# Seven block products at the end of batch 1, and variances by quarters, in a two-layer attention kernel

## The chip, the cores and the metric

The kernel runs on one core of one Trainium2 chip. The metric is the device time of one execution in microseconds (us), from the first to the last instruction of the program with what lies around them. A median of several runs is given. The engines are named as in the profile: PE multiplies matrices, PEld loads its weights, DVE and POOL work on tiles in SBUF, ACT evaluates activation functions, SP issues most of the DMAs. PE, DVE, ACT and POOL each execute their instructions in the order in which the program emits them. A DMA that SP issues waits in SP's own queue until its source is written.

## The reference

The input is x, two batches of 512 channels by 2048 tokens (64 x 32), in float32. Layer 0 is softmax attention with 8 heads over all tokens, an output projection and a residual. Layer 1 is landmark attention with a pseudoinverse, then a feed-forward map whose two matrices have no nonlinearity between them. Each half of layer 1 begins with a normalization over the channels and adds its result to what it got:

```python
def _ln_t(v, eps=1e-5):
    m = jnp.mean(v, axis=-1, keepdims=True)
    s = jnp.var(v, axis=-1, keepdims=True)
    return (v - m) / jnp.sqrt(s + eps)
...
x = _L0_conv_ref(x, Wq, Wk, Wv, Wout, bout)          # attention, projection, + x
t = _to_tokens(x)
t = t + _L1_attn_ref(_ln_t(t), Wqkv, Wout, bout, conv_w)
...
out = out @ Wout + bout                               # the end of _L1_attn_ref
...
t = t + _L1_ffn_ref(_ln_t(t), qidx, scales, W)
...
y = jnp.einsum('bsd,od->bso', x, w_lora)              # in _L1_ffn_ref
out = jnp.einsum('bsd,od->bso', y, W)
```

## The kernel before

Channels lie on partitions, as four chunks of 128 (KC = 4); tokens are worked on in four blocks of 512 (NTB = 4, TB = 512). The heads of a batch are four pairs (NPAIR = 4). A product of a 512x512 weight with a block of 512 tokens is 16 products of 128x128 with 128x512; each product in float32 leaves two matmul records and two weight loads in the profile.

The program goes through these stages, and each has its filler, work of another stage that is put between its steps so that PE has something to do while other engines answer.

1. Layer 0, `attention0`: eight pairs of heads. Steps are made in groups of two (`GROUP`): scores on PE, exponentials on ACT into a pool of six tiles (`ppool`), sums of them on DVE (L1307), values on PE. After given groups (`BURSTS`) the filler gets a burst; after others one small call is taken from the list `soon`. While the first pair of batch 1 runs, the filler is `finish0_units`, the end of batch 0: for each block of 512 tokens the output projection (`out0_units`, four units of four products, L1168, each evacuated by DVE at L1175 from one of two PSUM banks "pp"), then the steps of `norm0_steps`. Those are: sums over the channels on DVE, the mean by a product with a matrix of 1/512 on PE (L1190), the subtraction on DVE, squares on ACT, their sums on DVE, the variance by the same kind of product (L1206) with a square root on ACT (L1208); then, taken from `soon` after one group, the reciprocal on DVE (L1227), and from `soon` after the next group the two multiplications with it, one half on POOL (L1230) and one on DVE (L1231), and the store of the normalized block.
2. The end of batch 1 of layer 0 beside the first products of layer 1. The order is a string written out by hand, `ORDER`: m is a step of the products, n a step of the norms, o a unit of a projection. These products already are seven block products instead of eight (`Unit`, `products`).
3. Batch 1's products in layer 1, and values.
4. The main loop of layer 1 over eight pairs, batch 1's four first (n = 0 to 3), then batch 0's (n = 4 to 7). `pinv` makes five rounds on each pair, about 7.4 us of PE each (L1856, L1866) with DVE between (L1879), and calls `chunk(c)` after a round and `last(i)` six times at the end. Those hold the landmark attention of the pair after (`after`), the last attention of the pair before (`before`: `attn1_scores`, `attn1_values`, `attn1_sums`, `attn1_inverse`, `attn1_end`), and, from n = 4, units of `finish1_units`, which is the end of batch 1 in layer 1. For each block of 512 tokens that is: the projection (four units), the norm (`norm_units`, the same `statistics` as above, its reciprocal at L1988), and the map (`map_units`, four units of four products, L2022). The map works on the centred block; each of its results is multiplied by the inverse deviation (`rstd`) on DVE (L2011), added to the block (L2012) and stored from SP (L2013). `TURNS` says at which places a unit ("f") is taken; some of the generator's items are empty (`GAP`), and use a turn without any work. The fourth block is taken earlier on its own ("o").
5. The tail: the last pair's last attention (`last_attn1`), the end of batch 1 and that of batch 0 in the order of the string `TAIL` (1 is a step of the attention, f a unit of batch 1, a and b units of batch 0's first and second projection, s and t steps of their norms), and then batch 0's maps, with the norm of the next block between the units of the map of this one.

A softmax's denominators are already treated in quarters: `sums_of` (L805) puts sums over 512 columns as four products with 32 weights each on four quarters of the partitions, DVE takes the reciprocal of 128x256 instead of 128x512 (L1336, L1952), and `spread` copies the result back to all rows by eight small DMAs from SP (L816).

The copies in question:

```python
    def spread(dst, few):
        for h in range(2):
            for to in range(2):
                for j in range(2):
                    lo, src = h * D + to * Q, h * D + j * Q
                    nc.sync.dma_start(dst[lo : lo + Q, j * LM : (j + 1) * LM], few[src : src + Q, :])
```

## Time and profile before

| what | us |
|---|---|
| median of 3 runs (2648.84 to 2649.84) | 2648.89 |
| the profiled execution's own time | 2649.55 |
| its span, from the first to the last instruction | 2647.7 |
| PE idle from 690 to 900 (end of batch 0 in layer 0) | 0.0 of 210 |
| PE idle from 1350 to 1520 (the stage of `ORDER`) | 3.0 of 170 |
| PE idle from 2090 to 2480 (n = 4 to 7 of the main loop) | 4.4 of 390 |
| PE idle from 2480 to 2648 (tail) | 10.0 of 168 |
| DVE busy in the same four stretches | 135, 132, 210, 103 |

The busy share of PE is a union of records, and a record lasts longer than the time after which the next one may start: a 128x512 record takes 592 ns, and the next starts 429 ns after it. What a product costs where PE runs without a break is read from the starts of neighbouring records or weight loads, not from its duration. "Idle before" in a group is the time in which the engine had nothing just before these instructions, and the arrow names what ended it. SPq is the queue of SP, where a DMA's instruction has a duration of its own before the transfer has landed.

### The profile page before, as it was taken

How to read it: one execution, taken by the hardware profiler on the slowest of the kernel's cores; microseconds unless marked ns; L12 is line 12 of the kernel's file. 1: busy time of each engine (PE TensorE's matmuls, PEld its weight loads, DVE VectorE, ACT ScalarE, POOL GpSimd, SP SyncE). 2: the span in 40 equal slices, each digit the busy share in tenths (PEclk: the TensorE clock that was granted, in tenths of full speed). 3: DMA queues.
4: the chain of work that ended last, by engine and by line, in shares of the span. 5: the costliest groups of instructions: out<-in, count | busy, mean ns of one | idle time of the engine just before them, and what ended most of it. 6: DMA issues, size and time to landing. Idle time of an engine off the chain costs nothing.

```text
span 2647.7 us, 41440 instructions
## 1 busy us (share of the span) xinstructions
PE 2623.1 (99%) x16882; PEld 1353.3 (51%) x16882; DVE 1780.1 (67%) x2259; ACT 921.0 (35%) x1398; POOL 169.6 (6%) x127
## 2 busy tenths in 40 slices
PE   9999999999999999999999999999999999999998
PEld 5343443444344344353344555777677666665444
DVE  5788897886667778767867866544644645465665
ACT  1444453443344434435522323223333232231310
POOL 0011011000001100000002000000000000000000
PEclk9999999999999999999999999999999999999999
DMA  4011011201221201011115633213111112121211
GB/s 147 22 30 36 13 33 49 77 21 52 88 80 58 91 25 32 25 56 60 41 44 182 225 125 118 98 33 129 48 37 61 60 45 100 34 81 36 97 35 49
DMA packets 123608, 177.16 MB, mean 67 GB/s; under 512 B 16784, under 2 KB 77968, under 8 KB 120848
## 3 DMA queue, kind: packets, MB, share of 16 engines
q1 hardware_dynamic: 117264, 153.15, 17.8%
q0 software_dynamic: 5440, 20.97, 2.0%
q8 instruction: 134, 2.20, 0.4%
q14 instruction: 66, 0.54, 0.1%
q10 hardware_dynamic: 704, 0.31, 0.0%
HBM read 94.02 MB, written 63.57 MB: 60 GB/s over the span
## 4 chain that ended last, share of the span: by engine, by line
PE 91%; DVE 6%; issue 1%; ACT 1%; DMA 1%; SPq 0%; DVEq 0%; ACTq 0%
PE av_f L1319 15%; PE sc_f L1289 15%; PE pb L1866 5%; PE pa L1866 5%; PE vp_f L1153 4%; PE yp_g L1168 4%; PE yp_f L1168 4%; PE fp_g L2022 4%; PE vp L1153 4%; PE pc_f L1021 3%; PE pu L2207 3%; DVE acc_f L1307 3%; PE pu_f L1021 2%; PE sc L1695 2%; PE sc L1923 2%; PE av L1716 2%
## 5 line engine op out<-in xcount | busy, mean ns | idle before, releaser
L1297 ACT ACTIVATE p_f<-sc_f 128x1024 f32<-128x1024 f32 x512 | 496.5, 1021 | 540.2 <-PE sc_f L1289 540.0
L1307 DVE TENSOR_TENSOR acc_f<-acc_f,p_f 128x1024 f32<-128x1024 f32 x448 | 575.3, 1284 | 110.8 <-ACT p_f L1297 83.9
L1319 PE MATMUL av_f<-p_f,v_f 64*64 64x512 f32 x4096 | 494.4, 589 | 2.8 <-DVE q_f L1326 2.8
L1289 PE MATMUL sc_f<-q_f,k_f 64*64 64x512 f32 x4096 | 489.9, 591 | 0.3 <-ACT p_f L1297 0.3
L1319 PEld LDWEIGHTS av_f<-p_f,v_f 64*64 64x64 f32 x4096 | 162.5, 133 | 286.8 <-issue 274.3
L1289 PEld LDWEIGHTS sc_f<-q_f,k_f 64*64 64x64 f32 x4096 | 154.2, 133 | 282.2 <-issue 277.2
L1866 PE MATMUL pa<-M 128*128 128x192 f32 (+1 forms) x640 | 150.3, 380 | 0.0
L1866 PE MATMUL pb<-R 128*128 128x192 f32 (+1 forms) x640 | 149.3, 380 | 0.6 <-DVE M L1879 0.6
L1153 PEld LDWEIGHTS vp_f<-wv_f,x 128*128 128x128 f32 x1024 | 115.8, 192 | 5.5 <-issue 5.2
L1866 PEld LDWEIGHTS pb<-R 128*128 128x128 f32 x640 | 106.5, 190 | 23.6 <-DVE M L1879 0.8
L1866 PEld LDWEIGHTS pa<-M 128*128 128x128 f32 x640 | 108.2, 193 | 19.8 <-ACT M L1857 2.0
L1153 PE MATMUL vp_f<-wv_f,x 128*128 128x128 f32 x1024 | 117.9, 276 | 0.0
L1168 PE MATMUL yp_g<-o,wo_f 128*128 128x512 f32 x256 | 113.8, 595 | 0.0
L1168 PE MATMUL yp_f<-q_f,wo_f 128*128 128x512 f32 x256 | 112.4, 595 | 0.1
L1339 POOL TENSOR_TENSOR q_f<-q_f,rinv_f 128x512 f32<-128x512 f32 x32 | 49.0, 1530 | 970.1 <-DMA rinv_f<-acc_f 647.5
L1153 PE MATMUL vp<-w,xh 128*128 128x128 f32 x896 | 105.8, 276 | 0.0
L1153 PEld LDWEIGHTS vp<-w,xh 128*128 128x128 f32 x896 | 102.2, 192 | 5.4 <-issue 3.5
L1879 DVE SCALAR_TENSOR_TENSOR M<-M,pb 128x320 f32<-128x320 f32 (+1 forms) x160 | 60.1, 417 | 60.8 <-PE pb L1866 60.8
L2022 PE MATMUL fp_g<-xn_g,mT 128*128 128x512 f32 (+1 forms) x232 | 99.3, 579 | 0.0
L1928 ACT ACTIVATE p<-sc 128x512 f32<-128x512 f32 x128 | 66.7, 602 | 91.6 <-PE sc L1923 91.1
L1960 POOL TENSOR_TENSOR o<-o,rinv 128x512 f32<-128x512 f32 x32 | 44.4, 1386 | 772.9 <-DVE rinv L1959 587.5
L1879 DVE SCALAR_TENSOR_TENSOR R<-M,pa 128x320 f32<-128x320 f32 (+1 forms) x160 | 58.5, 407 | 42.1 <-PE pa L1866 42.1
(293 smaller groups left out, 3215.9 us busy)
## 6 DMA issues: line engine op xcount, KB each, us to landing
xh<-xh_fd SPq DMA_DIRECT2D x12, 1024.0 KB, 7.9
rinv_f<-acc_f SPq DMA_DIRECT2D x256, 32.0 KB, 1.9
xr_f<-in_x_dram SPq DMA_DIRECT2D x8, 1024.0 KB, 5.2
x_fd<-xr_f POOLq DMA_DIRECT2D x8, 1024.0 KB, 4.7
xh_fd<-xn_f POOLq DMA_DIRECT2D x8, 1024.0 KB, 4.4
k_fd<-kq SPq DMA_DIRECT2D x16, 512.0 KB, 2.6
q_fd<-kq SPq DMA_DIRECT2D x16, 512.0 KB, 3.2
k<-k_fd SPq DMA_DIRECT2D x8, 1024.0 KB, 6.0
```

The source lines that it names most:

```text
L1021: nc.tensor.matmul(to, lhsT=w[:, k, :], rhs=x[:, k, :], start=start and k == 0, stop=k == 1, skip_group_check=True,)
L1153: nc.tensor.matmul(vp[:, j * P : (j + 1) * P], lhsT=xb[:, k, j * P : (j + 1) * P], rhs=w_of(k), start=k == 0, stop=k == KC - 1,)
L1168: nc.tensor.matmul(yp, lhsT=wo_sb[:, k, m * P : (m + 1) * P], rhs=oTs[k][:, toks], start=k == 0, stop=k == NPAIR - 1,)
L1289: nc.tensor.matmul(sc[r * D : (r + 1) * D, h, :], lhsT=hd.k[rows, lo : lo + D], rhs=hd.q[rows, t * TB : (t + 1) * TB], start=True, stop=True,)
L1297: nc.scalar.activation(p, sc, AF.Exp, scale=D**-0.5)
L1307: nc.vector.tensor_tensor(acc, first if c == 1 else acc, p, ALU.add)
L1319: nc.tensor.matmul(av[r][half, :], lhsT=hd.v[keys, c, half], rhs=pp[keys, h, :], start=c == 0, stop=c == NST - 1,)
L1866: nc.tensor.matmul(dst, lhsT=lhsT[:, k, t * P : (t + 1) * P], rhs=rhs[:, k, :], start=k == 0, stop=k == 1)
L1879: nc.vector.scalar_tensor_tensor(out, m, scale, pr, ALU.mult, ALU.subtract)
L1928: nc.scalar.activation(p[:, h, :], sc, AF.Exp, scale=D**-0.5)
L2022: nc.tensor.matmul(fp[:, cols], lhsT=mT[:, k, m * P : (m + 1) * P], rhs=self.xn[:, k, cols], start=k == 0, stop=k == KC - 1,)
L2207: nc.tensor.matmul(to, lhsT=w[:, k, :], rhs=x[:, k, :], start=start and k == 0, stop=k == 1, skip_group_check=True)
```

## The change

The products. `finish1_units` no longer makes the projection of blocks 1 to 3 and the map of blocks 0 to 2 by 16 products of 128x128 with 128x512. It takes a 512x512 weight as two by two halves, the 512 tokens as two halves of 256, and makes seven products of halves instead of eight (`Seven`), each in two parts of the rows and two of the columns: 28 products of 128x128 with 128x256 for a block. For that it needs sums of halves of the weights (`sums_of_weight`, made once in layer 0, on DVE, and stored in HBM) and sums of halves of the tokens (eight subtractions of 128x256 on DVE for a block), which are put where finished tokens lay. A unit accumulates in one bank over four of the products and copies it by ACT between them, so that a product waits for a copy. The map of block 3, the projection of block 0 and all of batch 0 stay as they were.

The weights. The two weights and their sums no longer stay in SBUF in n = 4 to 6: the weight and its sums, 1 MB each, are loaded before each use into the same two buffers. At the start of n = 7 both weights and both sums are loaded, 4 MB, and stay.

The variances. In all 16 norms the product of 128x512 becomes four products with 32 weights on 128 columns each, the square root and the reciprocal work on 128x128, and 16 DMAs from SP copy the result to all rows (`inverse_deviation`). Where `norm0_steps` had the reciprocal and the multiplications in one step (stage 2), they are now two; in the end of batch 0 (stage 1) they were two already.

The orders. `ORDER`, `TURNS` and `TAIL` are new; block 2 of `finish1_units` begins only in n = 7. Followed through, the units of n = 4 to 6 are those of blocks 0 and 1, and n = 7 and the tail have blocks 2 and 3; the last four turns "f" of `TAIL` have nothing left to take.

```diff
-ORDER = "1omnonmmnomomnnm2mnoonmnmnmoomnnm3mnoonmnmmnoomnnmnmmmnmnmmmnmmmmnmnmmmm"
...
-TAIL = "11fffnf11f1ff1afafff1f1f1f1faas11bsbs11bbt"
+ORDER = "1ommmnonmnomnomnmm2nmmoonmnnmnomonmmmnm3mnoonnnmmnoonnnmmmmnnmnmmnmmmnmmmnmmmmmmn"
+
+TURNS = "010010000001010001001201|110020000000100001001013|210000000100100010011112|111112201100101011011101"
+
+OUTS = "000000000000000001000100"
+
+TAIL = "11fffn1ff1a1ffa1ffff11a11ffff1as1b1sbs1bbt"
...
+    def inverse_deviation(rstd, few):
+
+        nc.vector.reciprocal(few, few)
+        for j in range(4):
+            for to in range(4):
+                nc.sync.dma_start(
+                    rstd[to * Q : (to + 1) * Q, j * P : (j + 1) * P], few[j * Q : (j + 1) * Q, :]
+                )
...
-        var = bank(f"var_{name}")
-        nc.tensor.matmul(var, lhsT=mean_w, rhs=sq[:, 0, :], start=True, stop=True)
-        rstd = row()
-        nc.scalar.activation(rstd, var, AF.Sqrt, bias=eps, scale=1.0)
+        var, few = bank(f"var_{name}"), apool.tile([P, P], F32, tag="few", name=f"few_{name}", bufs=1)
+        for j in range(4):
+            nc.tensor.matmul(
+                var[j * Q : (j + 1) * Q, :P], lhsT=mean_w[:, :Q], rhs=sq[:, 0, j * P : (j + 1) * P],
+                start=True, stop=True,
+            )
+        nc.scalar.activation(few, var[:, :P], AF.Sqrt, bias=eps, scale=1.0)
...
-        nc.vector.reciprocal(rstd, rstd)
-        if halves:
-            yield
+        inverse_deviation(rstd, few)
+        yield
         nc.gpsimd.tensor_tensor(xn[:, 2:, :], xn[:, 2:, :], wide, ALU.mult)
         nc.vector.tensor_tensor(xn[:, :2, :], xn[:, :2, :], wide, ALU.mult)
...
+            lo, hi = slice(0, h), slice(h, TB)
+            u = (side_bank(3, f"pu_{name}") if self.split else bank(f"pu_{name}"))[:, :h]
+            c = bank(f"pc_{name}")[:, :h]
+            product(u, 1)
+            nc.scalar.copy(d[0][:, lo], u)
+            product(c, 2)
+            add(0, lo, c)
+            product(u, 6, False)
+            nc.scalar.copy(d[0][:, hi], u)
+            if self.split:
+                yield
+            b = bank(f"pb_{name}")[:, :h]
+            product(b, 5)
+            nc.scalar.copy(d[1][:, hi], b)
+            product(u, 7, False)
+            add(1, hi, u)
+            product(b, 3, False)
+            add(0, hi, b)
+            product(u, 4, False)
+            nc.scalar.copy(d[1][:, lo], u)
+            for i in range(2):
+                end(j + 2 * i, d[i])
+            yield
...
+        def map_sevens(self, w, sums):
...
+            def end(m, d):
+                xb, toks = self.xb, slice(self.t * TB, (self.t + 1) * TB)
+                nc.vector.tensor_tensor(d, d, self.rstd, ALU.mult)
+                nc.vector.tensor_tensor(xb[:, m, :], d, xb[:, m, :], ALU.add)
+                nc.sync.dma_start(chunked(out[self.b])[:, m, toks], xb[:, m, :])
...
+            w, sums = (block_of(*to, f"w{i}_{kind}_{t}") for i, to in enumerate(
+                ((lpool, "wo"), (mpool, "m")) if kind == 0 else ((mpool, "m"), (lpool, "wo"))
+            ))
+            nc.sync.dma_start(w, chunked(wo1) if kind == 0 else mT_d)
+            nc.sync.dma_start(sums, ws_d[kind])
+            return w, sums
...
+            if t == NTB - 2:
+                while after:
+                    yield GAP
...
+            if t:
+                pair = weights(0, t)
+            yield from gap(1 if t else 2)
+            yield from f.out_sevens(*pair) if t else f.out_units()
+            pair = weights(1, t)
             yield from f.norm_units()
-            yield from f.map_units(lambda m, name: bank(name))
+            yield from f.map_sevens(*pair)
...
+            wo_sb = load_wo(wo1, "wo_last")
+            mT = block_of(mpool, "m", "mT_last")
+            nc.sync.dma_start(mT, mT_d)
...
+            for i in range(2):
+                nc.sync.dma_start(last_sums[i], ws_d[i])
+            outs_early.append(early[0].out_sevens(wo_sb, last_sums[0]))
```

## The prediction

> **What bounds the kernel.** I read first the busy table and the slices: PE is busy 99% of the span at full clock in every slice, and the chain that ended last is PE to 91%.

> ```profile
> PE 2623.1 (99%) x16882; PEld 1353.3 (51%) x16882; DVE 1780.1 (67%) x2259; ACT 921.0 (35%) x1398; POOL 169.6 (6%) x127
> ...
> PE 91%; DVE 6%; issue 1%; ACT 1%; DMA 1%; SPq 0%; DVEq 0%; ACTq 0%
> ```

> So PE time that is taken away is gained one to one, and a wait that reaches PE is paid one to one; there is no slack to hide it. Then I read the groups by form for the operations that change, and SP's instructions and the timeline around one norm, because the change puts a transfer where an instruction was.

> ```profile
> L1227 DVE RECIPROCAL rstd_n<-rstd_n 128x512 f32<-128x512 f32 x8 | 26.7, 3336 | 0.0
> L1336 DVE RECIPROCAL acc_f<-acc_f 128x256 f32<-128x256 f32 x32 | 55.8, 1742 | 0.0
> ```

> ```profile
> 2469.56 4.95 SPq L816 DMA_DIRECT2D rinv<-acc  x8
> ```

> ```profile
> 742.75 3.34 DVE L1227 RECIPROCAL rstd_n<-rstd_n 128x512 f32<-128x512 f32 x1
> 746.01 4.46 DVE L1307 TENSOR_TENSOR acc_f<-acc_f,p_f 128x1024 f32<-128x1024 f32 x2
> 750.39 1.21 DVE L1231 TENSOR_TENSOR xn_f<-xn_f,rstd_n 128x1024 f32<-128x1024 f32 x1
> 751.52 2.54 DVE L1307 TENSOR_TENSOR acc_f<-acc_f,p_f 128x1024 f32<-128x1024 f32 x2
> 753.98 0.74 DVE L1175 SCALAR_TENSOR_TENSOR xr_f<-yp_f,b_f,xr_f 128x512 f32<-128x512 f32 x1
> ```

> ```profile
> 748.85 14.00 PE L1168 MATMUL yp_f<-q_f,wo_f 128*128 128x512 f32 x32
> ```

> The reader is to see that eight small copies hold SP for 4.95 us, 0.62 each (0.56 from the first to the second, then 0.634), and the last lands 1.85 after it is issued; and that on DVE the multiplication by rstd stands between the reciprocal and the evacuation (L1175) for which PE's projection needs a free bank.

> **The gains.** (a) A 128x512 record starts 0.429 after the one before. The last unit of the kernel is in 128x256, and its 15 weight loads take 3.21, 0.214 each. A block's 16 products cost 32 x 0.429 = 13.73, its 28 new ones 56 x 0.214 = 11.98; six blocks save 6 x 1.74 = 10.5. (b) A variance's two records hold PE 0.86. Four quarters on 256 columns (L805) hold it 0.59 (2466.29 to 2466.88); with 128 columns not more, and not less than half, 0.30. I take 0.40, nearer to the half, since only the columns halve: 16 x 0.46 = 7.4 saved (4.3 to 9.0). (c) At the end of the last pair (2458 to 2474) PE now idles 0.47, 0.39, 0.38, 0.18 and 0.79, where turns are empty; the new ones put three half units and a whole one there. I take 2. Together 19.9.

> DVE's shorter reciprocals are worth nothing by themselves, since PE doesn't wait for DVE. Their length goes by columns: 3336 for 512 and 1742 for 256 give about 0.95 for 128. What DVE (eight subtractions and eight additions of 0.42 a block) and ACT (eight copies of 0.37) get in addition lies beside a full PE. The sums of the weights are eight DVE instructions of 0.69 in layer 0, where DVE is free for 111 us of 604 (86 to 690): nothing.

> **The cost: rstd comes late.** In place of one reciprocal come a reciprocal of 0.95 and 16 copies behind each other on SP. From the reciprocal's end to rstd: 0.06 + 0.56 + 14 x 0.634 + 1.85 = 11.3; with the reciprocal 12.3, against 3.35 now. Who waits?

> (d) End of batch 0 in layer 0, 690 to 910; nothing moves in the order. The reciprocal, then ends at 743.7, rstd is there at 755.0. DVE stands at the multiplication from 746.3, with the two sums of the next group and the evacuation of the first projection unit behind it: 1.21 + 2.54 + 0.74, and 1.9 more, because POOL's half now runs at the same moment (two sums beside it take 4.46 instead of 2.54). The bank comes free at 761.4. PE needs it for the third unit at 748.85 + 6.86 = 755.7: it stands 5.7. The reciprocal is 6.1 ahead of the next projection at three places (742.75, 797.88, 849.58): 17. Behind the fourth (909.73) no projection comes, but SP's softmax copies stand ahead of it (to 914.8) and DVE stands some 11 before sums that free the six tiles of exponentials; the groups come every 3.43, so the third group after finds no tile. I take 3 (0 to 5). Together 20 (11 to 22).

> (e) End of the seventh pair. The variance of block 1 is in `last(2)`, both map units follow at once. From 2361.5: variance 0.4, a table load of 1.28 that the copies ahead of it no longer hide, root and reciprocal, copies from 2364.7, rstd at 2376.0. The first map unit ends on PE at 2368.6; DVE stands there until 2376.0, then has four endings of 0.69. The second unit's last product needs an addition behind them (2379.7 instead of 2374.7): 5. The softmax's eight copies queue behind the 16, so the next pair's start (L1830) has its inputs some 3 later than PE; today about 1 is lost. I take 7 (2 to 9).

> (f) Tail. Today 7.1 of map lie between the last pair's sums (2483.4) and the next scores. Now only a mean and the scores do, and the turn "a" needs `attn1_end` of block 0, which is there 10.6 after the sums (copy and reciprocal 2.3, eight copies 5.0 and the landing 1.3 more, DVE 0.7, POOL 1.3). PE has 0.9 + 2.0 + 2.6 of work until then, so 5 are idle, of which today's 1.5 (before the mean) are taken off: about 4 (0 to 6).

> (g) First block of batch 0 (2551): rstd at 2555.5 + 11.3 = 2566.8; then the first ending (1.38) and the sums of squares (2.0) stand ahead of the next variance, which PE reaches at 2566.0 and gets at 2570.2: 4. (h) The last block: rstd at 2626.8 + 11.3 = 2638.1, PE's last product is 1 us off; five endings, 3 x 1.38 + 2 x 0.88, finish at 2644.0 instead of 2641.28: 2.7. Blocks 1 and 2 have 14 of projection between: nothing.

> (i) In the stage of `ORDER`, about 13, 8.5, 9 and 12 of PE work lie between reciprocal and multiplication, counted by 1.72 a step m and 3.43 a unit o; two of them are 3 to 4 short, and half reaches PE: 2 (0 to 7). (j) Loads: 2 MB for block 1's projection have some 11 us; at the start of n = 7 three 1 MB loads must land in about 11, and a single one takes 5: 1 (0 to 8). (k) Inside a unit each copy (0.37, plus 0.3 on the way) has 0.86 of another product as cover, as long as ACT and DVE are free: 12 units, 1 (0 to 6).

> The sum: 20 + 7 + 4 + 4 + 2.7 + 2 + 1 + 1 = 41.7 lost, 19.9 gained, +22. The profiled execution took 2649.55 (1.85 around its span), 0.66 above the median: 2671.

> [...]

> **Rivals.** *The copies are issued faster.* They are half the spread's size, and other DMAs hold SP for 0.32 (k_fd, 128 rows). At 0.37 a copy rstd comes after 7.3 and (d) shrinks to 6, (e) to 1, (g), (h) and (i) to nothing: 20 - 14 = 6 gained, 2643, faster. The change turns from loss to gain at about 0.43 a copy. Against it: none of the spread's copies, which have 32 rows too, is below 0.507. *The weights come late.* If the loads of n = 7 queue behind each other at 5 us each, PE stands another 8 there: 2679. For it: 4 MB and two more in one queue; against it: four 1 MB loads at 1182 landed within 14 us. *Seven products save nothing*, if each of the 12 units waits 0.9 for a copy or an addition: 2681. Against it: the same scheme at 1370 to 1510 runs with little idle time.

> **How the numbers follow.** Forecast 0.60, faster copies 0.20, late weights 0.10, no saving 0.10. The range goes from the faster rival's edge to the slow ends of (i) to (k) on the forecast: 2643 to 2687. 0.2% (5.3 us) is about what can be told from no change: faster 0.16 (of the first rival's 0.20), same 0.07 (the rest of it and 0.03 of the forecast's lower end), slower 0.77.

> **What would show it.** Right: about 0.6 between copies on SP; three waits of PE at the projection of layer 0 of 4 to 6, released by DVE; a wait of DVE for rstd of 7 in the seventh pair; DVE ending after PE at the close by 5; weight loads of 0.214 in `Seven`. Wrong: copies at 0.4 or less, or PE without idle time from 690 to 910.

## The result, and the profile after

The changed kernel takes 2736.63 us (median of 5 runs, 2733.01 to 2739.39), the kernel before beside it 2649.63: ratio 1.0328, 95% interval 1.0314 to 1.0342. That is 87 slower; forecast were 2671 and at most 2687. The profiled execution took 2733.01, with a span of 2731.1, against 2647.7; it is the lowest of the five, at a mean granted clock of 0.985, while the other four ran at 0.983 or 0.984.

The busy table and the chain of the changed kernel:

```profile
PE 2638.1 (97%) x17122; PEld 1384.8 (51%) x17122; DVE 1787.5 (65%) x2351; ACT 933.9 (34%) x1446; POOL 171.4 (6%) x127
...
PE 80%; DVE 9%; SPq 5%; DMA 3%; issue 2%; ACT 1%; DVEq 0%; ACTq 0%
```

PE was 91% of the chain and is 80%. The rest went to DVE, to SP's queue and to DMAs, none of which had more than 6%. PE's busy time rose, although the change takes work from PE: a first sign that this work ran slower.

The groups by form show that the reciprocal became as short as it was expected to be (0.95):

```profile
L1183 DVE RECIPROCAL few_g<-few_g 128x128 f32<-128x128 f32 x8 | 7.6, 949 | 10.5 <-ACT few_g L1218 10.5
L1183 DVE RECIPROCAL few_n<-few_n 128x128 f32<-128x128 f32 x8 | 7.5, 937 | 0.0
```

The timeline of the changed kernel around the same norm as that shown of before (start, length, engine, line; in square brackets the idle time ahead of it and what ended it):

```profile
750.62 0.94 DVE L1183 RECIPROCAL few_n<-few_n 128x128 f32<-128x128 f32 x1
...
751.60 10.23 SPq L1186 DMA_DIRECT2D rstd_n<-few_n  x16
...
756.73 7.13 PE L1166 MATMUL yp_f<-q_f,wo_f 128*128 128x512 f32 x16
...
763.33 1.23 DVE L1240 TENSOR_TENSOR xn_f<-xn_f,rstd_n 128x1024 f32<-128x1024 f32 x1 [9.36 <-DMA rstd_n<-few_n]
763.55 3.21 POOL L1239 TENSOR_TENSOR xn_f<-xn_f,rstd_n 128x1024 f32<-128x1024 f32 x1 [45.17 <-DMA rstd_n<-few_n]
764.48 4.69 DVE L1316 TENSOR_TENSOR acc_f<-acc_f,p_f 128x1024 f32<-128x1024 f32 x2
...
769.09 1.40 DVE L1173 SCALAR_TENSOR_TENSOR xr_f<-yp_f,b_f,xr_f 128x512 f32<-128x512 f32 x2
769.88 5.30 PE L1166 MATMUL yp_f<-q_f,wo_f 128*128 128x512 f32 x6 [6.02 <-DVE xr_f L1173]
```

The 16 copies hold SP for 10.23, 0.6 each from start to start after the first. From the reciprocal's end (751.56) to the multiplication are 11.8 (forecast 11.3). DVE stands 9.36 at it, its two sums take 4.69 beside POOL, the evacuation comes behind them, and PE stands 6.02 (forecast 5.7). The last line has what was not forecast: its 6 records take 0.88 each, where 32 took 14.00 before, 0.44 each. The windows around this wait (PE's busy time comes second, PEclk is the granted clock):

```profile
core 0: us, PE busy (x) PEld busy (x) DVE busy (x) ACT busy (x) POOL busy (x), PEclk, DMA share, GB/s
758.00:764.00 6.00, 5.87 (x14) 2.28 (x12) 0.67 (x1) 0.00 (x0) 0.45 (x1) 1.00 0.08 22
764.00:768.00 4.00, 0.00 (x0) 0.00 (x0) 3.90 (x3) 0.00 (x0) 3.57 (x2) 1.00 0.00 0
768.00:774.80 6.80, 4.92 (x6) 2.18 (x7) 2.49 (x3) 0.00 (x0) 0.00 (x0) 0.50 0.38 154
774.80:790.00 15.20, 15.20 (x84) 5.71 (x83) 10.99 (x10) 3.88 (x4) 1.44 (x2) 1.00 0.24 87
```

Four us after PE fell idle the granted clock drops to 0.50 and stays there for 6.8, of which PE works 4.92. Such stretches follow waits at ten other places of this kernel. Before had one alone, behind PE's last product.

The longest waits of PE in the changed kernel (total, number, longest):

```profile
PE yp_f L1166 <- DVE xr_f L1173: 18.0, 3, 6.3
PE pu_f_g L2034 <- ACT d_f_g L2046: 11.3, 2, 6.6
PE av_f L1328 <- DVE q_f L1335: 10.7, 6, 4.0
PE sc_f L1298 <- ACT p_f L1306: 8.1, 2, 7.8
PE var_g L1214 <- DVE sq_g L1210: 5.6, 1, 5.6
PE p_pb L1879 <- DVE R L1902: 3.3, 1, 3.3
PE var_n L1214 <- DVE xr_f L1173: 3.2, 1, 3.2
```

To see where the 83.4 of span went, both traces were cut at the same exponentials (the nth of the 512 in layer 0, the nth of the 132 in `attn1_scores`), and in each piece PE's idle time and its busy time at clock 0.5 were summed, before / after:

| piece of before, us | difference | PE idle | PE busy at 0.5 |
|---|---|---|---|
| 0 to 684 | +0.7 | 5.9 / 5.8 | 0 / 0 |
| 684 to 1057, end of batch 0 in layer 0 | +50.3 | 0.0 / 33.7 | 0 / 33.3 |
| 1057 to 1346 | -0.7 | 0.4 / 0.4 | 0 / 0 |
| 1346 to 1755, with the stage of `ORDER` | +7.5 | 3.2 / 11.0 | 0 / 0 |
| 1755 to 2193 | -1.7 | 1.5 / 0.8 | 0 / 0 |
| 2193 to 2357 | +2.3 | 0.6 / 4.8 | 0 / 5.1 |
| 2357 to 2463, seventh and last pair | +9.8 | 0.6 / 13.6 | 0 / 6.8 |
| 2463 to 2534, tail | +4.0 | 3.3 / 4.6 | 0 / 3.4 |
| 2534 to PE's end | +9.4 | 0.0 / 7.1 | 0 / 6.2 |
| behind PE's end | +1.8 | | |

Idle time is 66 of it. 54.8 of work at half clock took twice as long as it need have: 27.4. The end is 1.8. What is left, 12, is the gain.

### The profile page after: what moved, and what is told of

The parts are those of the page before. It is cut to its first block, busy times and chain, and to the rows that moved or that the text cites. A ratio compares the mean times of both kernels' runs of the same rounds, so it can differ in the third digit from the quotient of the medians.

```text
span 2731.1 us, 42485 instructions
## 1 busy us (share of the span) xinstructions
PE 2638.1 (97%) x17122; PEld 1384.8 (51%) x17122; DVE 1787.5 (65%) x2351; ACT 933.9 (34%) x1446; POOL 171.4 (6%) x127
## 3 DMA queue, kind: packets, MB, share of 16 engines
q8 instruction: 136, 2.23, 0.3%
## 4 chain that ended last, share of the span: by engine, by line
PE 80%; DVE 9%; SPq 5%; DMA 3%; issue 2%; ACT 1%; DVEq 0%; ACTq 0%
PE av_f L1328 13%; PE sc_f L1298 13%; PE pb L1889 4%; PE vp_f L1151 4%; PE pa L1889 4%; PE vp L1151 4%; DVE acc_f L1316 4%; SPq L1186 3%; PE pc_f L1019 3%; PE yp_f L1166 3%; PE pu L2383 3%; PE pu_f L1019 2%; PE yp_g L1166 2%; PE sc L1718 2%; PE av L1739 2%
## 5 line engine op out<-in xcount | busy, mean ns | idle before, releaser
L1166 PE MATMUL yp_f<-q_f,wo_f 128*128 128x512 f32 x256 | 120.3, 625 | 18.1 <-DVE xr_f L1173 18.0
L1166 PEld LDWEIGHTS yp_f<-q_f,wo_f 128*128 128x128 f32 x256 | 50.4, 200 | 84.7 <-issue 63.1
L2389 ACT COPY kq<-pu 128x512 f32<-128x512 f32 x56 | 32.2, 586 | 151.8 <-PE pu L2383 122.8
```

What stands on the lines that cost most here:

```text
L1166: nc.tensor.matmul(yp, lhsT=wo_sb[:, k, m * P : (m + 1) * P], rhs=oTs[k][:, toks], start=k == 0, stop=k == NPAIR - 1,)
```

## The experiments

**Theory A**, after the comparison: the 16 copies make rstd late, PE stands for it, and each long stand is followed by a stretch of half clock. **Rival B**: the loss is in the waits inside the seven products and in their weights. **Rival C**: the half clock has a cause of its own, such as a denser load of the array. In the expectations below TensorE is PE, VectorE DVE, ScalarE ACT and GpSimd POOL.

**1. The old variance in the changed kernel.**

```
-        for j in range(4):
-            nc.tensor.matmul(
-                var[j * Q : (j + 1) * Q, :P], lhsT=mean_w[:, :Q], rhs=sq[:, 0, j * P : (j + 1) * P],
-                start=True, stop=True,
-            )
-        nc.scalar.activation(few, var[:, :P], AF.Sqrt, bias=eps, scale=1.0)
+        nc.tensor.matmul(var, lhsT=mean_w, rhs=sq[:, 0, :], start=True, stop=True)
+        nc.scalar.activation(few, var, AF.Sqrt, bias=eps, scale=1.0)
...
-        nc.vector.reciprocal(few, few)
-        for j in range(4):
...
+        nc.vector.reciprocal(rstd, rstd)
```

> The changed kernel with the variance as it was (one product of 512 columns, one root, one reciprocal of 128x512, no copies); the seven products, the sums and the orders stay. Theory A (the 16 copies make rstd late, TensorE stands for it, and after each long stand the granted clock is 0.5 for a while): what is left is the gain of the products and of the better filled end of the last pair, 10.5 + 2, and the stall at 694 us behind the store of the map's sums, 3.9 and half of the 6.8 at half clock behind it: 2649.6 - 12.5 + 7.3 = 2644; half clock only at about 693 and at the end. Rival B (the loss lies in the waits inside the seven products and in the late weights): stays above 2700. Rival C (the half clock has another cause than the waits, such as the denser load of the array): about 34 us of lost clock stay, 2678.

Measured 2679.46, ratio 1.0114 (1.0099 to 1.0130). 57 of the 87 go, which speaks against B, but 29 stay: A alone is not enough. The time is the one that C named (2678), but not for C's reason: 24.4 of work ran at half clock, so 12.2 were lost and not 34. The trace has 6 stretches of half clock in place of 12, again each behind a wait. The waits that stay: 3.90 at 694, 4.00 at 949 (VectorE has the sums of the output projection's weights there), 4.36 at 1474 in the stage of `ORDER`, and 3.78 at 2466 in the last pair's inverse. The stage of `ORDER` loses 9.5 here, cut as in the table above, although rstd is early again: the new `ORDER` has a price of its own. The stall at 694 in the changed kernel's timeline:

```profile
686.20 0.34 SPq L1440 DMA_DIRECT2D ws_fd<-ws_f  x1
...
691.54 1.13 DVE L1465 MEMSET rows<- 128x1288 f32 x1 [5.36 <-DMA ws_fd<-ws_f]
...
694.39 2.83 PE L1328 MATMUL av_f<-p_f,v_f 64*64 64x512 f32 x10 [3.92 <-DVE q_f L1335]
```

The new store of the map's sums reads the tile that `write_bands` (it writes the bands of the convolution) clears next. DVE stands 5.36 for the store, with the addition that PE needs behind it.

**2. The quarters alone**: the kernel before with the changed `statistics`, `inverse_deviation` and `ORDER`, and 16 products as they were.

> The kernel before with nothing of the change but the variances by quarters, their 16 copies and the changed ORDER of batch 1 in layer 0, which gives rstd a step of its own. Theory A: the end of batch 0 in layer 0 loses what the changed kernel lost there without the stall at 694 (50 - 7 = 43), the stage of ORDER 7, and the ends of layer 1 some 15 to 25 (the seventh pair, the first and the last block): 2649.6 + 43 + 7 + 20 = 2720 (2710 to 2730), with stretches of half clock at about 768, 830, 891, 960 and 983. Rival B: the quarters bring their 7.4 and little else, 2642 to 2655. Rival C: the waits without the half clock, about 2685.

Measured 2724.09, ratio 1.0282 (1.0268 to 1.0296): +74, A, of which 10.5 lie in the stage of `ORDER`. PE stands 5.84, 5.86 and 6.49 at the three projections and 8.57 behind them, then 3.30 and 2.71 in the stage of `ORDER`, 6.59 in the tail and 3.96 before block 1's variance. Idle time grew by 52.7, PE worked 43.5 at half clock, the end grew by 3.7: 52.7 + 21.8 + 3.7 = 78.2 for a span longer by 73.7. So the quarters give PE about 4.5.

**3. The old variance, and the bands written later**, so that no memset stands behind the store.

```
             wo_sb = loaded.pop()
-            write_bands()
+        if n == NPAIR + 2:
+            write_bands()
```

> As the run with the old variance, and the bands of the convolution are written three pairs later, so that their memset no longer stands behind the store of the map's sums in the tile that both use. Theory A: the stall of 3.9 at 694 and the half clock behind it go, 7.3 less than with the old variance alone: 2637, with no half clock but that at the end. Rival B: above 2700. Rival C: 2670, half clock without long waits.

Measured 2673.95, ratio 1.0093 (1.0079 to 1.0107). The stall at 694 and its half clock are gone, 5.5 of the 7.3 that they were priced at. The level of 2637 is missed for the reason found in run 1: the waits at 943, 1469 and 2461 are there as before.

**4. Four copies in place of sixteen.**

```
         for j in range(4):
-            for to in range(4):
-                nc.sync.dma_start(rstd[to * Q : (to + 1) * Q, j * P : (j + 1) * P], few[j * Q : (j + 1) * Q, :])
+            nc.sync.dma_start(rstd[:, j * P : (j + 1) * P], few[j * Q : j * Q + 1, :].unsqueeze(1).to_broadcast([1, P, P]))
```

> The changed kernel with 4 copies in place of the 16: each takes one row of a quarter and writes it to all 128 rows. Theory A: if such a copy holds its queue 0.63 and lands 1.85 after, rstd is there 0.95 + 0.06 + 0.56 + 2 x 0.63 + 1.85 = 4.7 after the reciprocal starts, 1.3 later than before the change, in place of 11.4. TensorE's three waits at the end of batch 0 shrink from 6 to 0 to 2 and no half clock follows them: 2649.6 - 19.9 + 7.3 (694) + 3 to 10 = 2640 to 2647. If a copy from one row is slow, it lies between that and 2737, and the waits say by how much. Rival B: above 2700 whatever the copies take. Rival C: 2670 or more.

Measured 2709.15, ratio 1.0219 (1.0205 to 1.0233). The timeline, and the row of DMAs (number, KB each, median from issue to landing):

```profile
751.67 2.75 SPq L1185 DMA_DIRECT2D rstd_n<-few_n  x4
```

```profile
rstd_n<-few_n SPq DMA_DIRECT2D x32, 64.0 KB, 6.8
```

SP is held 2.75 by the four, 0.69 a copy (0.63 expected). But a copy out of one row into 128 lands after 6.8, not 1.8; rstd is there 9.3 after the reciprocal's end in place of 11.8, and the three waits of PE are 3.55, 3.54 and 3.53 in place of 6.0, 5.7 and 6.3. 2.5 less delay gave 2.2 to 2.7 less waiting: the waits follow the delay, whatever the number of copies.

**5. Longer work of VectorE in the kernel before**, with no copy at all: pairs of reciprocals that cancel, behind that of rstd.

```
+            for n in ((P,), (2 * P,), (2 * P, P), ())[t]:
+                nc.vector.reciprocal(rstd[:, :n], rstd[:, :n])
+                nc.vector.reciprocal(rstd[:, :n], rstd[:, :n])
```

> The kernel before; behind the reciprocal of rstd in the first three blocks of batch 0 in layer 0 stand two more reciprocals, which cancel, of 128, 256 and 256 + 128 columns: 1.9, 3.5 and 5.4 us of VectorE, about 1.0 of which has cover. No copy is added. Theory A (a stand of TensorE is followed by half clock only if it is long, whatever causes it): TensorE stands 0.9, 2.5 and 4.4 at the second unit of the three projections; the last, and only the last, is followed by 3.4 to 6.8 at a granted clock of 0.5; 2649.6 + 7.8 + 2 to 3.4 = 2660. Rival C (the half clock belongs to the copies or to the changed products): the three waits and no half clock, 2657. Every wait followed by it: 2667.

Measured 2661.00, ratio 1.0039 (1.0026 to 1.0052). PE stood 0.75, 2.35 and 4.33. Windows around the second and the third:

```profile
814.00:817.00 3.00, 1.19 (x3) 0.68 (x4) 2.42 (x3) 0.00 (x0) 0.00 (x0) 1.00 0.84 347
817.00:820.40 3.40, 3.40 (x5) 1.35 (x4) 0.00 (x0) 0.00 (x0) 0.00 (x0) 0.50 0.01 2
...
868.00:871.60 3.60, 1.48 (x4) 0.38 (x2) 3.60 (x3) 0.00 (x0) 0.85 (x2) 1.00 0.00 0
871.60:878.40 6.80, 4.59 (x6) 2.02 (x7) 2.71 (x4) 0.00 (x0) 0.36 (x1) 0.50 0.38 154
```

A wait is enough, without the copies and without the change: C falls. The wait of 0.75 is followed by nothing, that of 4.33 by 6.8 at 0.50, and against the expectation that of 2.35 by 3.4. It is not so in every execution: of the five runs, two took 2658.9 and 2658.7 at a mean granted clock of 0.999, that of the kernel before, and the profiled one 2662.4 at 0.997.

**6. The sums elsewhere, in the changed kernel**: those of the output projection one pair and eight turns later, the bands two pairs later.

```
-        if n == NPAIR + 1:
+        if n == NPAIR + 2:
             wo1_sb = block_of(lpool, "xr", "wo1_f")
...
-            soon.extend([lambda: next(wo1_sums)] * 2)
+            soon.extend([lambda: None] * 8 + [lambda: next(wo1_sums)] * 2)
```

> The changed kernel; the sums of the output projection's weights are made one pair later in layer 0 and eight turns into it, and the bands are written two pairs later, away from the store of the map's sums. Theory D (the sums of the weights, which the prediction costed at nothing, cost two stalls with half clock behind each): the stall at 694 (3.9 + 3.4) and the one at 984 (4.0 + part of the 10.2 at half clock) go: 2736.6 - 7.3 - 8.5 = 2721. If the second stall is that of the late rstd and not of the sums, only the first goes: 2729.

Measured 2728.24, ratio 1.0301 (1.0285 to 1.0317): 8.4 less than the changed kernel. The stall at 694 is gone; of that at 984, 2.23 of 4.0 stay, with half clock behind. So the weight sums cost some 8 in the changed kernel (the two profiled executions differ by 4.5 only, since 57.4 of work ran at half clock in this one against 54.8), and the rest of the second stall is the late rstd's: run 2, without any such sums, has 2.37 there.

**7. The seven products alone**: old variance, old `ORDER`, and the sums where run 6 put them.

> The seven products alone: the variance and ORDER as before the change, the sums of the weights and the bands away from each other as in the run before. Theory A + D: the stage of ORDER loses the 9.4 that it had with the old variance and the new ORDER, layer 0 the 8.5 of the second sums: 2674 - 17.9 = 2656, what is left being waits in layer 1 (VectorE's sums and subtractions ahead of the last pair's inverse 3.8 + 3.4, the changed TAIL some 6) less the 12 that the products save. If the products save nothing: 2668.

Measured 2657.95, ratio 1.0028 (1.0017 to 1.0040). As A with the sums expects (2656). Layer 0 is as before. The stage of `ORDER` loses 0.5, against 9.5 in run 1. The waits that are left are in layer 1: 1.41 and 0.79 + 0.82 in the seventh pair, 3.88 in the last pair's inverse, 1.22, and 1.46 + 1.58 in the tail; behind 0.79 + 0.82, 3.88 and 1.46 + 1.58 come stretches of 3.4, 3.4 and 6.8 at half clock.

**8. The subtractions one turn later.**

```
             next(steps)
+            yield GAP
             for call in calls[2:]:
                 call()
-            yield from gap(2)
+            yield GAP
```

> As the run before, and the second two of the four subtractions of the map's sums come one turn later, no longer in one turn with the sums of squares ahead of the last pair's inverse. The wait of 3.8 in that inverse shrinks by their 1.5 to 2.3, too short for half clock: 2656 - 1.5 - 3.4 = 2651. If the wait only moves with them: 2656.

Measured 2658.32, ratio 1.0030 (1.0018 to 1.0041): nothing gained. In the last pair that turn has no other work between it and the one before, so the two came out back to back again. The timeline of VectorE there:

```profile
2440.20 0.69 DVE L1973 TENSOR_TENSOR rinv<-av,rinv 128x512 f32<-128x512 f32 x1 [1.80 <-issue]
2440.81 2.35 DVE L1204 TENSOR_TENSOR sq_g<-sq_g,sq_g 128x512 f32<-128x512 f32 x2
...
2445.14 0.74 DVE L1893 SCALAR_TENSOR_TENSOR R<-M,pa 128x320 f32<-128x320 f32 x2
```

VectorE first stands 1.80 for the softmax's copies, then works off the sums beside POOL (2.35 for two), and the inverse's step at 2445.14, for which PE waits 4.38, comes last.

**9. The old `ORDER` with the late rstd.**

```
-                if step in (1, 3) and t:
+                if step == 2 and t:
...
         inverse_deviation(rstd, few)
-        yield
+        if halves:
+            yield
```

> The changed kernel with ORDER as it was before, reciprocal, copies and multiplication of rstd in one step again. It tells whether the 7.4 that the changed kernel lost in the stage of ORDER come from the new ORDER or from the late rstd. If from the late rstd: VectorE now stands 11 at each of the four multiplications, with its sums for TensorE's products behind it, and each such stand of 3 and more is followed by half clock: 10 to 30 more than the changed kernel, 2747 to 2767. If from the new ORDER, which lost 9 with the old variance too: 7 less, 2729.

Measured 2766.76, ratio 1.0442 (1.0426 to 1.0458): with the old `ORDER` the late rstd costs 30 more. The waits in that stage are 6.87, 7.14, 9.04 and 10.06. The new `ORDER` avoids most of this, and still loses 7.5. That these 7.5 are the late rstd's is not shown: with the early rstd of run 1 the new `ORDER` loses 9.5.

**10. The sums of squares first.** Run 8, and in the last pair the turn stands ahead of `attn1_end`; the two subtractions come a chunk later.

```
+            first = n == NPAIR + 3 and c == NTB - 1
+            if first:
+                turn(c, 0)
             if before and 0 < c <= n_ones:
                 before.attn1_end(c - 1)
...
-112201100101011011101"
+112201100100021011101"
```

> The seven products with the old variance and ORDER and the sums elsewhere (2658), and in the last pair the sums of squares stand ahead of VectorE's multiplication by the softmax's sums, for whose copies it waited 1.8, and the last two subtractions come one chunk later. The wait of 4.4 in the inverse shrinks to about 0.6 and the 3.4 to 6.8 at half clock behind it go: 2658 - 3.8 - 2.5 = 2652. If the wait has another cause, such as the softmax's copies, it stays: 2658.

Measured 2651.81, ratio 1.0004 (0.9995 to 1.0013). The same place now:

```profile
2438.05 1.28 DVE L1204 TENSOR_TENSOR sq_g<-sq_g,sq_g 128x512 f32<-128x512 f32 x2
2439.37 0.69 DVE L1205 TENSOR_TENSOR sq_g<-sq_g 128x512 f32<-128x512 f32 x1
2439.98 0.68 DVE L1973 TENSOR_TENSOR rinv<-av,rinv 128x512 f32<-128x512 f32 x1
2440.58 0.74 DVE L1893 SCALAR_TENSOR_TENSOR R<-M,pa 128x320 f32<-128x320 f32 x2
```

The sums fill the time in which VectorE stood; the wait of 4.38 is 0.60, and the half clock behind it is gone. Both moves were made at once; what each is worth was not told apart. This is the best version with seven products, 85 better than the changed kernel and no different from before. Its span is 2.3 longer: idle time +9.7, 6.8 more of work at half clock (3.4), an end shorter by 2.2. So the products give about 8.6, and the waits of layer 1 eat it.

**11. The copies on GpSimd.**

```
-                nc.sync.dma_start(
+                nc.gpsimd.dma_start(
```

> The changed kernel with the 16 copies issued by GpSimd in place of SP. By the rows of before, GpSimd is held 0.75 to 0.81 by each store of a block, of 512 rows of 2 KB in place of 32 rows of 512 B, and such a store lands 4.4 to 4.7 after its issue: if a small copy costs the same, the sixteenth lands 16 x 0.78 + some 2 = 14 after the reciprocal, 3 later than on SP, and GpSimd's own multiplication stands behind them: 2745 to 2765. If the hold goes with the rows it is far shorter than SP's 0.59, TensorE's waits at the projections vanish and what is left is the two stalls of the weight sums and the last pair: 2665 to 2680. [...]

Measured 2718.61, ratio 1.0262 (1.0245 to 1.0279): between the two expectations, 18 less than on SP.

```profile
751.33 7.88 POOL L1186 DMA_DIRECT2D rstd_n<-few_n  x16 [33.48 <-DVE few_n L1183]
...
760.36 1.23 DVE L1240 TENSOR_TENSOR xn_f<-xn_f,rstd_n 128x1024 f32<-128x1024 f32 x1 [6.93 <-DMA rstd_n<-few_n]
```

A copy holds GpSimd 0.49 and lands 1.6 later; rstd is there 9.3 after the reciprocal's end (751.02), and PE waits 3.60, 3.77 and 4.31.

**12. The copies on two queues.**

```
-                nc.sync.dma_start(
+                (nc.sync if to < 2 else nc.scalar).dma_start(
```

> The changed kernel with 8 of the 16 copies issued by SP and 8 by ScalarE. Theory A (TensorE's waits follow the time from the reciprocal to rstd): rstd is there 0.06 + 0.56 + 6 x 0.63 + 1.85 = 6.3 after the reciprocal in place of 11.3, if ScalarE is free; ScalarE is held 4.7, beside exponentials that TensorE needs every 3.43. The three waits of 6 shrink to 1 to 2, those of the layer's end by 3 to 5, and half clock behind them goes: some 9 places x 5 = 45 less, 2690 (2680 to 2710). If the copies hold ScalarE when TensorE waits for its exponentials, that comes back: 2720. If the copies share one path to the memory, so that two queues are no faster than one: 2737.

Measured 2733.94, ratio 1.0317 (1.0300 to 1.0334): nothing gained.

```profile
750.46 5.16 SPq L1186 DMA_DIRECT2D rstd_n<-few_n  x8
750.46 5.47 ACTq L1186 DMA_DIRECT2D rstd_n<-few_n  x8
756.31 1.94 ACT L1306 ACTIVATE p_f<-sc_f 128x1024 f32<-128x1024 f32 x2 [7.46 <-DMA rstd_n<-few_n]
```

The two queues do run side by side, 0.65 to 0.68 a copy, and the waits at the projections vanish. But ScalarE issues copies for 5.47 while the exponentials wait, and PE stands 5.73, 5.31, 5.53 and 6.00 for those. It is the second outcome that was named, and dearer than it was put there (2720). The time is nearer to the third (2737), but the timeline rules that one's reason out, since the two queues work at the same time.

## Why the prediction was wrong

The mechanism of the main cost was right: the 16 copies at 0.6, rstd 11 late, PE behind DVE. The size failed at two steps that stood at nothing, and at smaller ones.

- **The price of a wait.** The prediction paid waits "one to one". That step failed: behind the longer ones PE went on at half clock (behind the 6.02 at 764, 6.8 at 0.50). 54.8 of work ran so, 27.4 lost, the largest part of the 62 by which the profiled execution exceeds the forecast. Run 5 shows it without the change.
- **"The sums of the weights ... nothing"** failed. DVE's free time in layer 0 was counted for the whole layer, not for the places where the sums stand, and the store's hold on a shared tile was not looked at. 3.9 and 4.0 of idle time stand at their two places, of which 2.2 are the late rstd's; run 6 prices the sums at some 8 together with their half clock.
- **(i), `ORDER`**: 2 forecast, 7.8 of idle time found, just beyond its upper end of 7. DVE stands 3.10 for rstd there, with the sums behind it for which PE then waits 3.2. Two more waits, 1.6 and 2.7, come behind reductions of 4.6 on DVE, and the trace does not tell how much of them is rstd's. The prediction priced the lateness alone and not the new order: run 1 loses 9.5 in this stage without the lateness, run 7 with the old order 0.5. Run 9 shows what the lateness costs in the old order.
- **(d)**: three waits 18.0 (17 forecast), right. Behind the fourth block 7.8, not 3: DVE stood 13.8, for the copies as forecast behind the softmax's, and then its sums took 4.69 beside POOL.
- **(e)**: 7 forecast, 6.6 measured: DVE stands 8.05 for rstd, and PE for the copy of the second unit behind it. A wait of 4.6 one norm earlier (2292) was not forecast. In the trace a copy of ScalarE stands behind one that waits 6.9 for a store in SP's queue, behind the softmax's copies, and those behind the 16. Run 1, without copies, has no such wait there; no run isolates it further.
- **(f), (c)**: PE idles 3.3 in the last pair's inverse and 1.3 more in the tail, about the 4 of (f), but that is luck, for (f)'s reason is not the cause: runs 7, 8 and 10 show that the first comes of VectorE's sums ahead of the inverse. Those sums were put "beside a full PE"; the inverse hands each step from PE to DVE and back, and there DVE's delay reaches PE.
- **(g)** 4 forecast, 5.6; **(h)** 2.7, and the end grew by 1.8. Both near.
- **(j)**, late weights: no wait of PE for them in the trace. **(k)**: 3.0 of waits in run 10 (1.41 and 1.64) in place of 1.
- **(a)** 10.5 forecast, 8.6 by run 10; **(b)** 7.4 (4.3 to 9.0), 4.5 by run 2, though a variance's records hold PE 0.42 as assumed (0.40). Where the rest of (b) went was not found.

Against the forecast these are 27.4 for the clock, 7.9 at the places of the sums, 5.8 for (i), 5.8 for (d), 4.6 for the wait at 2292, 1.6 for (g) and some 6 of gains that didn't come (12 of 17.9): 59 of the 62. By runs: run 2's 74, run 6's 8.4 and run 7's 7.7 add up to 90, against 87: the three causes are nearly all. Run 2 holds the new `ORDER` too; without that stage's 10.5 it has 63, and the lateness of rstd is still far the largest. Of the rivals, faster copies did not come on SP. GpSimd at 0.49 was nearest to the turning point of 0.43 that the prediction gave, but with the half clock even that was slower than before by 69.

## What to carry to other kernels

Where PE has no slack, list each new wait of PE with its length, and price the long ones at their length plus half of the work at low clock behind them: here a wait of 6.02, with 4.92 of work at 0.50 behind it, cost 8.5. By the counts of the next section (an estimate from one trace) a wait of 1.3 to 4.5 may or may not bring such a stretch: here 3.33 did and 3.19 did not. Two executions of one kernel can differ by it (run 5: 2658.7 at a clock of 0.999, 2662.4 at 0.997). To shorten an instruction on an engine that has slack and pay with a transfer on the path lost here; it is the time to the result that counts, and 16 small copies behind each other cost 11.8 us of it here. Free time of an engine is to be counted at the place where the work is put, not over a stage, and a new store keeps its tile from whoever writes it next (a memset of DVE stood 5.36 for the store of the map's sums).
